# Reordering the prologue of a two-layer attention kernel, and spreading four sums over two units of products

## The chip, the cores and the metric

The kernel runs on one core of a Trainium2 chip. The metric is the device time of one execution in microseconds (us); the time of the kernel before is the median of three runs. Engines are named as in the profile: PE is TensorE (matrix products; PEld its weight loads), DVE is VectorE, ACT is ScalarE, POOL is GpSimd, and SP is the engine that issues most transfers (DMA). A "q" behind an engine's name (SPq, ACTq) is its queue of issued transfers.

## The reference

x has 8 images of 512 channels and 32x32 = 1024 positions, all in float32. Two attention layers follow each other. Cut to what matters:

```python
# layer 0: eight heads of 64 channels
hn  = group_norm(x, gn1_scale, gn1_bias)                 # 32 groups
qkv = einsum('bchw,oc->bohw', hn, w_qkv) + b_qkv         # 1536 x 512 weights
wgt = softmax(einsum('bct,bcs->bts', q * scale, k * scale))
a   = einsum('bts,bcs->bct', wgt, v)
out = group_norm(einsum('bchw,oc->bohw', a, w_proj) + b_proj, gn2_scale, gn2_bias)
x   = x + out
# layer 1: one head of 512 channels
w_qkv = g_qkv[:, None] * v_qkv / norm(v_qkv, axis=1)     # rows normalised
w_out = g_out[:, None] * v_out / norm(v_out, axis=1)
qkv = einsum('oc,bcn->bon', w_qkv, x)
qkv = qkv / (sqrt(mean(square(qkv), axis=1)) + 0.0001)
attn = softmax(einsum('bci,bcj->bij', q, k) * C ** -0.5)
h   = einsum('oc,bcn->bon', w_out, einsum('bij,bcj->bci', attn, v))
return (x + h) * 2 ** -0.5
```

## The kernel before

Channels lie on the 128 partitions in four blocks (ci = 0 to 3), so one image is a tile of 128 x 4 x 1024. The program is written out in full: the order of the calls is the order on each engine (class InOrder pins it), and each engine takes its own instructions strictly in that order. Buffers are the other thing that orders work. Seven large buffers are handed out by name (class Slots: a buffer given back goes to the end of a list, and the next taker waits for its last readers). The products' results go to PSUM: wide() gives one of three tiles of two banks, bank() one of two tiles of one bank, each in turn, and a new taker waits until the former result has been copied out. Each issued transfer also carries one of eight completion counters, and waits until the transfer that had this counter before has landed.

Layer 1 never forms q, k, v as such. Weights that do not depend on x are multiplied together once, in the prologue:

- score = wq' wk (product "pA", 16 products of 128x128 by 128x512, each done by PE in two passes), value = wv' wo' (product "pB", needs the transposed output weight woT), and gram = the sum over the 12 row tiles of w_qkv of rows' rows ("pG", upper blocks only: widths 512, 384, 256, 128), from which the mean square of qkv follows.
- score, value and layer 0's output weight are then cut into seven operands each (operands(): four sums on DVE, three copies on POOL, two transfers to a place in device memory, "far"), for a scheme that does a 2x2 block product with seven products in place of eight (class Seven).

The rows of layer 1's weights ("wrows", 16 tiles of 128x512: q, k, v, out) have to be normalised first: ACT squares a tile and sums it ("w"), DVE takes the inverse root by thirteen small steps (rsqrt_steps), multiplies it with g, and scales the tile.

Layer 0's weights come as rows and must be transposed (turn(): 16 products with the identity into two wide PSUM tiles, "wT_", half of each copied by DVE and half by ACT). The vectors (scales and biases) are loaded as rows of one small tile, and turned with one product ("pcol") into "cols".

The prologue before runs in this order: statistics of image 0 and its norm; turn v's weights (wT_v); half of v's projection (pv); turn k's and q's weights; first q and k projection (pqk), with the squares and the scaling of the w rows between; score (pA); turn woT; value (pB); operands; turn the projection (wT_p); its operands; gram (pG); store gram and fetch it again. Then the first scores of layer 0 ("s") begin. The loads are issued on SP: x, layer 0's rows, layer 1's rows in four transfers of 1 MB, the projection; the vectors on ACT.

For each image the heads of layer 0 follow (32 steps), its projection, and then layer 1: the products with gram (py), u = score times x (p_u, scaled on POOL by the inverse of the root mean square), v in four units of seven products (value_unit, p_v), and e, the exponents, in four units (weight_unit, p_e). weight_unit needs four sums of quarters of u (sum_u, tiles s12 and s34). A unit's products go in pairs into one wide tile, and after each second product Seven.drain() issues the additions that empty it. In the kernel before, sum_u puts its four sums on DVE in one go after the second of the four v units.

Of the kernel before, what the change touches and what calls it, by code (L numbers as in the profile page):

```python
# [8 lines left out]
F32 = mybir.dt.float32  # L9
# [43 lines left out]
def attention_blocks_kernel(  # L53
# [52 lines left out]
    def big(name, lead=CI):  # L106

        return slots.take([P, lead, CI * N // lead], name)
# [14 lines left out]
    def run(pieces):  # L123
        for _ in pieces:
            pass
# [10 lines left out]
        for hh in range(2):  # L136
            SY.dma_start(out=w0rows[t][hh * D : (hh + 1) * D], in_=w0v[t, hh])

    rows = const.tile([NCOLS, P], F32, name="rows")
    for r0, vec in (  # L140
        (G1S, gn1_scale), (G1B, gn1_bias), (BP, b_proj), (G2S, gn2_scale), (G2B, gn2_bias),
        (GQKV, g_qkv), (GOUT, g_out),
    ):
        n = vec.shape[0] // P
        AC.dma_start(out=rows[r0 : r0 + n, :], in_=vec.rearrange("(r p) -> r p", p=P))

    bv = b_qkv.rearrange("(j hh t d) -> t j hh d", hh=2, t=3, d=D)
    for t in range(3):
        for hh in range(2):
            AC.dma_start(out=rows[BQ + 4 * t : BQ + 4 * t + 4, hh * D : (hh + 1) * D], in_=bv[t, :, hh, :])  # L150

    def load_x(b, xt, ci):
        SY.dma_start(out=xt[:, ci, :], in_=xv[b, :, ci, :])
# [2 lines left out]
        load_x(0, x0, ci)  # L156
    for t in (2, 1, 0):
        load_w0(t)
    qk_rows, vo_rows = big("w1_qk", 2 * CI), big("w1_vo", 2 * CI)
    v1v = v_qkv.rearrange("(t j p) c -> t p j c", t=3, p=P)  # L160
    SY.dma_start(out=qk_rows[:, :CI, :], in_=v1v[0])
    SY.dma_start(out=qk_rows[:, CI:, :], in_=v1v[1])
    SY.dma_start(out=vo_rows[:, :CI, :], in_=v1v[2])
    SY.dma_start(out=vo_rows[:, CI:, :], in_=v_out.rearrange("(j p) c -> p j c", p=P))
    SY.dma_start(out=wprow, in_=w_proj.rearrange("(j p) c -> p j c", p=P))


    ident = const.tile([P, P], F32, name="ident")
# [62 lines left out]
    def fetch(name, b):  # L231
        SY.dma_start(out=place(name, b), in_=far[name])
# [488 lines left out]
    class Layer1:  # L721
# [10 lines left out]
        def project(self):  # L732
# [64 lines left out]
            def value_unit(m):  # L797

                w = near["value"]
                c = {f"{i + 1}{th + 1}": v[:, m + 4 * th, i * CH : (i + 1) * CH] for i in range(2) for th in range(2)}  # L800

                def last(which):
                    if which[0] == "1":
                        t = m + 4 * (which == "12")
                        AC.activation(v[:, t, :], v[:, t, :], AF.Copy, scale=rinv[:, t : t + 1])

                return Seven(
                    f"v_{b}_{m}", CH,
                    lambda k, h: w[:, k, h, :], self.right(slice(m * P, (m + 1) * P)), c, last, swap=True,
                )  # L810

            def sum_u():

                s12 = prob.tile([P, 2, 2, HN], F32, tag="p", name=f"s12_{b}")
                s34 = prob.tile([P, 2, 2, HN], F32, tag="p", name=f"s34_{b}")
                q1, q2 = halves_
                VE.tensor_add(s12[:, 0], u[:, :2, q2], u[:, 2:, q2])
                VE.tensor_sub(s12[:, 1], s12[:, 0], u[:, :2, q1])
                VE.tensor_sub(s34[:, 0], u[:, :2, q1], u[:, :2, q2])
                VE.tensor_sub(s34[:, 1], u[:, 2:, q1], s12[:, 1])  # L820
                self.s12, self.s34 = s12, s34
                for th in range(2):
                    e[th] = big(f"e_{b}_{th}", NT)
                    self.sums[th] = sum_pool.tile([P, HN], F32, tag="esum", name=f"esum_{b}_{th}")

            def weight_unit(m):

# [26 lines left out]
                        broadcast()  # L854
            if b + 1 < B:
                fetch("qk", b + 1)
            for m in range(4):
                run(value_unit(m).steps())
                if m == 1:
                    sum_u()  # L860
            if b + 1 < B:
                fetch("v", b + 1)
            for m in range(4):
# [25 lines left out]
                SY.dma_start(out=ov[self.b, :, c, :], in_=self.xt[:, c, :])  # L889


    place("qk", 0)
    place("v", 0)

    def turn_w0(t, name):
        near_t, far_t = (near["v"], far["v"]) if t == 2 else (near["qk"][:, t], far["qk"][:, t])
        turn(w0rows[t], near_t, name)
        SY.dma_start(out=far_t, in_=near_t)

    norm1 = Norm1(0, x0)  # L900
    for ci in range(CI):
        for k in range(2):
            norm1.stats(ci, k)
    pcol = bank("pcol", NCOLS)
    PE.transpose(pcol, rows, ident[:NCOLS, :NCOLS])
    VE.tensor_copy(cols, pcol)
    VE.tensor_scalar_mul(bqs, cols[:, BQ : BQ + CI], QSCALE0)
    VE.tensor_sub(bpd, cols[:, BP + 2 : BP + 4], cols[:, BP : BP + 2])
    norm1.means()
    norm1.gn.coeffs()  # L910
    for ci in range(CI):
        norm1.apply(ci, AC if ci % 2 else VE)
    turn_w0(2, "v")
    v0_0 = big("v0_0", NT)
    v0 = project_v0(0, x0, v0_0)
    for _ in range(NT // 2):
        next(v0)
    turn_w0(1, "k")
    turn_w0(0, "q")

    wrows = [qk_rows[:, j, :] for j in range(2 * CI)] + [vo_rows[:, j, :] for j in range(2 * CI)]
    nrm = [small.tile([P, 2 * CI], F32, tag="wn_n", name=f"wn_{k}") for k in range(2)]
    ss = [small.tile([P, 2 * CI], F32, tag="wn_ss", name=f"wss_{k}") for k in range(2)]

    def norm_rows(k):

        rsqrt(nrm[k], ss[k], 2 * CI, f"w1_{k}")
        VE.tensor_mul(nrm[k], nrm[k], cols[:, GQKV + 8 * k : GQKV + 8 * (k + 1)])
        for i in range(2 * CI):
            wrow = wrows[2 * CI * k + i]  # L930
            VE.tensor_scalar(wrow, wrow, nrm[k][:, i : i + 1], None, ALU.mult)

    qk0, todo = project_qk(0, 0, x0)
    for k in range(CI):
        next(todo)
        for i in range(CI * k, CI * (k + 1)):
            sq = prob.tile([P, C], F32, tag="p", name=f"w1_{i}")
            AC.activation(sq, wrows[i], AF.Square, accum_out=ss[i // 8][:, i % 8 : i % 8 + 1])
        if k % 2:
            norm_rows(k // 2)  # L940

    def prep_layer1():


        slots.give("rows_kq")
        woT = rows_vp[:, :CI, :]
        done1 = big("done1", 2 * CI)
        score, value = done1[:, :CI, :], done1[:, CI:, :]
        wq, wk, wv, wo = (wrows[k * CI : (k + 1) * CI] for k in range(4))

        def product(left, right, ci, c0, name):
            pm = bank(f"{name}_{ci}")
            run(matmuls(pm[:, c0:], [(l[:, ci * P : (ci + 1) * P], r[:, c0:]) for l, r in zip(left, right)]))
            return pm

        for ci in range(CI):
            VE.tensor_scalar_mul(score[:, ci, :], product(wq, wk, ci, 0, "pA"), QSCALE1)
        turn(vo_rows[:, CI:, :], woT, "o")
        for ci in range(CI):
            AC.copy(value[:, ci, :], product(wv, [woT[:, o, :] for o in range(CI)], ci, 0, "pB"))  # L960
        def operands(name, w, s7):

            q = [[w[:, 2 * j : 2 * j + 2, i * CH : (i + 1) * CH] for j in range(2)] for i in range(2)]
            op = [s7[i // 4][:, i % 4] for i in range(7)]
            VE.tensor_add(op[S1], q[1][0], q[1][1])
            VE.tensor_sub(op[S2], op[S1], q[0][0])
            VE.tensor_sub(op[S3], q[0][0], q[1][0])
            VE.tensor_sub(op[S4], q[0][1], op[S2])
            for i, part in ((A11, q[0][0]), (A12, q[0][1]), (A22, q[1][1])):
                PO.tensor_copy(op[i], part)  # L970
            SY.dma_start(out=far[name][:, :4], in_=s7[0])
            SY.dma_start(out=far[name][:, 4:], in_=s7[1][:, :3])

        for name, w, pool, tag in (("score", score, block, "pb"), ("value", value, prob, "p")):
            operands(name, w, [pool.tile([P, 4, 2, CH], F32, tag=tag, name=f"{name}7_{i}") for i in range(2)])
        slots.give("done1")
        done2, done3 = big("done2", 2 * CI), big("done3", 2 * CI)
        gram, proj = done2[:, :CI, :], done2[:, CI:, :]
        turn(wprow, proj, "p")
        d3 = done3.rearrange("p (k h) c -> p k (h c)", k=2).rearrange("p k (i h c) -> p k i h c", h=2, c=CH)  # L980
        operands("proj7", proj, [d3[:, k] for k in range(2)])

        VE.memset(gram, 0.0)
        for ci in range(CI):
            c0 = ci * P
            pg = product(wrows[: 3 * CI], wrows[: 3 * CI], ci, c0, "pG")
            VE.tensor_copy(gram[:, ci, c0 : c0 + P], pg[:, c0 : c0 + P])
            if c0 + P < C:
                VE.tensor_scalar_mul(gram[:, ci, c0 + P :], pg[:, c0 + P :], 2.0)
        SY.dma_start(out=far["gram"], in_=gram)  # L990
        SY.dma_start(out=far["proj"], in_=proj)
        for name in ("w1_qk", "w1_vo", "rows_vp", "done2", "done3"):
            slots.give(name)
        fetch("gram", 0)

    prep_layer1()


    heads = Heads(0, x0, v0_0, qk0)
# [133 lines left out]
```

## Time and profile before

| what | us |
|---|---|
| median of three runs | 3317.47 (3316.73 to 3318.27) |
| the profiled execution, its time | 3316.36 |
| its span (first to last instruction) | 3314.5 |
| PE busy | 3267.3 |
| DVE busy | 2117.2 |
| ACT busy | 1068.9 |
| POOL busy | 981.4 |
| first useful product of PE (wT_v) starts at | 16.56 |
| first scores (s) of layer 0 start at | 116.7 |

The span is a little shorter than the time; the difference, 1.9 us, lies around the program. A group's line gives the number of instructions, their busy time and mean, and the idle time of the engine just ahead of them with what ended it. A product's end is modelled (products overlap), so where the rate of PE matters, the distance between starts is used. The view of waits lists who waited for whom; the chain of waits follows the work that ended last back from step to step; the timeline gives start, duration and engine of each instruction in order. Nearly all instructions show one line, L34, since the recording class issues them all; they are told apart by the names of their tiles.

### The profile page before, as it was taken

Reading aid. Unit: us, or ns where it says so; the run is one execution under the profiler, and the core shown is the slowest. Engines: PE = TensorE matmul, PEld = TensorE weight load, DVE = VectorE, ACT = ScalarE, POOL = GpSimd, SP = SyncE. Lnnn points to the kernel's source line nnn. Section 1 sums busy time; section 2 is a strip of 40 time slices with the busy share of each in tenths; the row PEclk is TensorE's granted clock in tenths of the full one; section 3 lists DMA queues with packets and bytes.
Section 4 is the critical chain, followed back from the end, with each engine's and each line's share of the span. In section 5 each row is a group of like instructions: output and inputs, shape, how many; then the busy total and the mean of one; then the engine's idle time right before and its main releaser. Section 6 shows DMA issues by size and latency. Waiting matters only on the chain.

```text
span 3314.5 us, 35553 instructions
## 1 busy us (share of the span) xinstructions
PE 3267.3 (99%) x13177; PEld 1610.2 (49%) x13177; DVE 2117.2 (64%) x2830; ACT 1068.9 (32%) x1811; POOL 981.4 (30%) x855
## 2 busy tenths in 40 slices
PE   7999999999999999999999999999999999999899
PEld 3544544445444454544545445444454445444354
DVE  4596646965479654885448854497545966468653
ACT  2353123521145211451125512254122531235210
POOL 0253123521235112450224502254022531235111
PEclk9999999999999999999999999999999999999999
DMA  5586205752068410783117821287103862057600
GB/s 187 158 212 193 77 13 149 198 171 77 0 186 203 154 52 18 202 218 112 45 45 209 223 74 45 64 221 220 63 27 111 208 186 89 13 134 197 184 7 26
DMA packets 182659, 411.86 MB, mean 124 GB/s; under 512 B 27444, under 2 KB 27480, under 8 KB 176344
## 3 DMA queue, kind: packets, MB, share of 16 engines
q1 hardware_dynamic: 182368, 409.58, 43.5%
q8 instruction: 105, 1.72, 0.2%
q14 instruction: 66, 0.54, 0.0%
q10 hardware_dynamic: 120, 0.02, 0.0%
HBM read 113.53 MB, written 27.56 MB: 43 GB/s over the span
## 4 chain that ended last, share of the span: by engine, by line
PE 89%; DVE 4%; DMA 4%; SPq 2%; issue 1%; ACT 0%; DVEq 0%; POOL 0%; POOLq 0%
PE po L34 25%; PE s L34 12%; PE pqk L34 12%; PE pv L34 7%; PE p_e_T L34 7%; PE p_e_B L34 5%; PE py L34 4%; DMA pT<-pb 4%; PE p_u_T L34 3%; PE p_o_T L34 3%; PE p_v_T L34 3%; PE p_u_B L34 2%; PE p_o_B L34 2%; PE p_v_B L34 2%; DVE pb L34 2%; SPq L34 2%
## 5 line engine op out<-in xcount | busy, mean ns | idle before, releaser
L34 ACT ACTIVATE p<-s,nm 128x1024 f32<-128x1024 f32 x512 | 565.5, 1109 | 862.0 <-DVE nm L34 826.6
L34 POOL TENSOR_SCALAR p<-p,tt 128x1024 f32<-128x1024 f32 x512 | 565.9, 1118 | 927.6 <-DVE tt L34 924.2
L34 DVE TENSOR_REDUCE nm<-s 128x1 f32<-128x1024 f32 x512 | 602.2, 1218 | 175.0 <-PE s L34 174.3
L34 DVE STREAM_TRANSPOSE pb<-p 128x2048 f32<-128x2048 f32 x256 | 589.5, 2303 | 26.1 <-POOL p L34 16.4
L34 PE MATMUL s<-qk 64*128 64x512 f32 x2048 | 508.6, 602 | 0.0
L34 PE MATMUL po<-pT,v 128*64 128x256 f32 x4096 | 470.3, 382 | 4.7 <-DMA pT<-pb 3.5
L34 PE MATMUL pqk<-hn,qk 64*128 64x512 f32 (+1 forms) x2016 | 474.2, 591 | 0.0
L34 PE MATMUL po<-e,v 128*128 128x512 f32 x1024 | 450.9, 595 | 0.0
L34 PEld LDWEIGHTS po<-pT,v 128*64 128x64 f32 x4096 | 287.2, 137 | 216.6 <-ACT v L34 69.0
L34 PEld LDWEIGHTS pqk<-hn,qk 64*128 64x128 f32 (+1 forms) x2016 | 203.6, 187 | 250.2 <-issue 237.2
L34 PEld LDWEIGHTS po<-e,v 128*128 128x128 f32 x1024 | 192.2, 190 | 252.7 <-issue 245.5
L34 PEld LDWEIGHTS s<-qk 64*128 64x128 f32 x2048 | 195.0, 186 | 237.2 <-issue 231.3
L34 POOL TENSOR_TENSOR u<-u,xy 128x512 f32<-128x512 f32 x64 | 78.9, 1272 | 767.2 <-DMA xy<-far_rinv 590.4
L34 PE MATMUL pv<-v,hn 128*128 128x512 f32 x512 | 231.1, 603 | 1.4 <-ACT v L34 1.4
L34 DVE TENSOR_TENSOR e<-e,p_e_T 128x512 f32<-128x512 f32 x160 | 107.1, 686 | 145.0 <-PE p_e_T L34 142.8
L34 POOL TENSOR_TENSOR qk<-qk,v 128x512 f32<-128x512 f32 x124 | 158.4, 1277 | 83.9 <-ACT v L34 83.9
L34 ACT ACTIVATE e<-e,shift,rinv 128x512 f32<-128x512 f32 x128 | 100.9, 812 | 247.7 <-DVE e L34 247.7
L34 POOL TENSOR_TENSOR esum<-esum,e 128x512 f32<-128x512 f32 x96 | 121.5, 1266 | 164.0 <-ACT e L34 161.4
L34 PEld LDWEIGHTS pv<-v,hn 128*128 128x128 f32 x512 | 95.4, 192 | 118.2 <-issue 116.4
L34 PE MATMUL p_e_T<-s,t 128*128 128x512 f32 x320 | 147.8, 592 | 0.0
L34 PE MATMUL py<-x,gram 128*128 128x512 f32 x320 | 141.2, 601 | 6.0 <-issue 6.0
L34 DVE TENSOR_TENSOR v<-po,esum 128x512 f32<-128x512 f32 x56 | 38.7, 691 | 160.0 <-PE po L34 159.8
(184 smaller groups left out, 3059.0 us busy)
## 6 DMA issues: line engine op xcount, KB each, us to landing
pT<-pb SPq DMA_DIRECT2D x1024, 256.0 KB, 4.5
hn<-in_x_dram SPq DMA_DIRECT2D x32, 512.0 KB, 5.6
x<-in_x_dram SPq DMA_DIRECT2D x32, 512.0 KB, 5.9
out_dram<-x SPq DMA_DIRECT2D x32, 512.0 KB, 3.8
score<-far_score SPq DMA_DIRECT2D x8, 1792.0 KB, 7.4
value<-far_value SPq DMA_DIRECT2D x8, 1792.0 KB, 7.1
qk<-far_qk SPq DMA_DIRECT2D x7, 2048.0 KB, 7.8
proj<-far_proj SPq DMA_DIRECT2D x7, 1792.0 KB, 7.9
```

The lines of the kernel that those rows point to most:

```text
L34: return lambda *args, **kw: self._pin(call(*args, **kw))
```

## The change

In the prologue the order becomes: layer 1's rows are loaded first, in sixteen transfers of 256 KB, with only the two g vectors ahead on ACT; then x, layer 0's rows and the projection. The 16 row tiles are squared, normalised and scaled in five groups (2, 2, 4, 4, 4), and after each group PE adds its rows' part to all four blocks of gram, which are held in two wide PSUM tiles at once. The other vectors are loaded by ACT after the squares. Then come statistics of x, the turning of woT, score (pA) with the coefficients of the norm between, the turning of v's weights, value (pB), the turning of k's, v's projection, the turning of q's and of the projection, and the first q and k projection. So each turned weight is ready one stage ahead of its products. The norm is applied by POOL and DVE instead of ACT and DVE, score is copied from PSUM by ACT instead of DVE, the memory set of gram comes at the start, and gram stays where it is made: it is still stored, but not fetched.

In layer 1 the four sums of u are issued one by one, ahead of the additions of four different pairs, in the third and the fourth v unit.

The diff, cut to its core:

```diff
+    qk_rows, vo_rows = big("w1_qk", 2 * CI), big("w1_vo", 2 * CI)
+    wrows = [qk_rows[:, j, :] for j in range(2 * CI)] + [vo_rows[:, j, :] for j in range(2 * CI)]
+    g_rows = block.tile([4 * CI, P], F32, tag="pb", name="g_rows")
+    AC.dma_start(out=g_rows[: 3 * CI, :], in_=g_qkv.rearrange("(r p) -> r p", p=P))
+    AC.dma_start(out=g_rows[3 * CI :, :], in_=g_out.rearrange("(r p) -> r p", p=P))
...
+    for j in range(4 * CI):
+        SY.dma_start(out=wrows[j], in_=v1v[j] if j < 3 * CI else vov[j - 3 * CI])
...
-    SY.dma_start(out=qk_rows[:, :CI, :], in_=v1v[0])
-    SY.dma_start(out=qk_rows[:, CI:, :], in_=v1v[1])
-    SY.dma_start(out=vo_rows[:, :CI, :], in_=v1v[2])
-    SY.dma_start(out=vo_rows[:, CI:, :], in_=v_out.rearrange("(j p) c -> p j c", p=P))
...
-                VE.tensor_add(s12[:, 0], u[:, :2, q2], u[:, 2:, q2])
-                VE.tensor_sub(s12[:, 1], s12[:, 0], u[:, :2, q1])
-                VE.tensor_sub(s34[:, 0], u[:, :2, q1], u[:, :2, q2])
-                VE.tensor_sub(s34[:, 1], u[:, 2:, q1], s12[:, 1])
...
+                VE.tensor_add(s12[:, 0], u[:, :2, q2], u[:, 2:, q2])
+                yield
+                VE.tensor_sub(s12[:, 1], s12[:, 0], u[:, :2, q1])
+                yield
+                VE.tensor_sub(s34[:, 0], u[:, :2, q1], u[:, :2, q2])
+                yield
+                VE.tensor_sub(s34[:, 1], u[:, 2:, q1], s12[:, 1])
...
+            sums = sum_u()
             for m in range(4):
-                run(value_unit(m).steps())
-                if m == 1:
-                    sum_u()
+                for k, _ in enumerate(value_unit(m).steps()):
+                    if (m, k) in ((2, 0), (2, 4), (3, 1), (3, 5)):
+                        next(sums, None)
...
+    gram = place("gram", 0)
...
+    pcol = bank("pcol_g", 4 * CI)
+    PE.transpose(pcol, g_rows, ident[: 4 * CI, : 4 * CI])
+    VE.tensor_copy(cols[:, GQKV:], pcol)
...
+    VE.memset(gram, 0.0)
+    for lo, hi in ((0, 2), (2, 4), (4, 8), (8, 12), (12, 16)):
+        for i in range(lo, hi):
+            sq = prob.tile([P, C], F32, tag="p", name=f"w1_{i}")
+            AC.activation(sq, wrows[i], AF.Square, accum_out=ss[:, i : i + 1])
+        rsqrt(nrm[:, lo:hi], ss[:, lo:hi], hi - lo, f"w1_{lo}")
+        VE.tensor_mul(nrm[:, lo:hi], nrm[:, lo:hi], cols[:, GQKV + lo : GQKV + hi])
+        for i in range(lo, hi):
+            VE.tensor_scalar(wrows[i], wrows[i], nrm[:, i : i + 1], None, ALU.mult)
+            for ci in range(CI if i < 3 * CI else 0):
+                c0 = ci * P
+                PE.matmul(
+                    pg[ci][:, c0:], wrows[i][:, c0 : c0 + P], wrows[i][:, c0:], start=(i == 0), stop=(i == 3 * CI - 1)
+                )
+    load_vectors()
     norm1 = Norm1(0, x0)
...
+    norm1.aggregate()
+    pcol = bank("pcol", GQKV)
+    PE.transpose(pcol, rows, ident[:GQKV, :GQKV])
+    coeffs = norm1.gn.all_steps()
+    next(coeffs)
+    for ci in range(CI):
+        c0 = ci * P
+        VE.tensor_copy(gram[:, ci, c0 : c0 + P], pg[ci][:, c0 : c0 + P])
+        if c0 + P < C:
+            VE.tensor_scalar_mul(gram[:, ci, c0 + P :], pg[ci][:, c0 + P :], 2.0)
+    SY.dma_start(out=far["gram"], in_=gram)
+    VE.tensor_copy(cols[:, :GQKV], pcol)
...
+    turn(vo_rows[:, CI:, :], woT, "o")
+    for ci in range(CI):
+        AC.activation(score[:, ci, :], product(wq, wk, ci, "pA"), AF.Copy, scale=QSCALE1)
+        if ci == 1:
+            next(coeffs)
+            next(coeffs)
+    run(coeffs)
     turn_w0(2, "v")
+    for ci in range(CI):
+        norm1.apply(ci, PO if ci % 2 else VE)
+    operands("score", score, ...)
+    for ci in range(CI):
+        AC.copy(value[:, ci, :], product(wv, [woT[:, o, :] for o in range(CI)], ci, "pB"))
...
+    turn_w0(1, "k")
     v0_0 = big("v0_0", NT)
     v0 = project_v0(0, x0, v0_0)
     for _ in range(NT // 2):
         next(v0)
-    turn_w0(1, "k")
     turn_w0(0, "q")
+    operands("value", value, ...)
+    turn(wprow, proj, "p")
     qk0, todo = project_qk(0, 0, x0)
+    run(todo)
...
+    operands("proj7", proj, [d3[:, k] for k in range(2)])
+    SY.dma_start(out=far["proj"], in_=proj)
...
-        for ci in range(CI):
-            c0 = ci * P
-            pg = product(wrows[: 3 * CI], wrows[: 3 * CI], ci, c0, "pG")
...
-        fetch("gram", 0)
```

## The prediction

> **What bounds the kernel now.** I read the page's busy times first, then what TensorE waited for, in the whole span and in its first 122 us, then the chain of waits over that stretch, and last the timeline of one layer-1 stage.
>
> ```profile
> PE 3267.3 (99%) x13177; PEld 1610.2 (49%) x13177; DVE 2117.2 (64%) x2830; ACT 1068.9 (32%) x1811; POOL 981.4 (30%) x855
> ```
>
> TensorE (PE) is busy for all but 47 us, so time can only come from what it waits for. Its waits in the first 122 us (waited for: us, times, longest), with the layer-1 line from the whole span:
>
> ```profile
> PE pcol L34 <- DMA rows<-in_L_conv_b_qkv_dram: 10.5, 1, 10.5
> PE p_v_B L34 <- DVE v L34: 5.8, 8, 0.7
> PE wT_v L34 <- DMA rows_vp<-in_L_conv_w_qkv_dram: 2.1, 1, 2.1
> PE pA L34 <- DVE done L34: 1.5, 1, 1.5
> PE pv L34 <- ACT v L34: 1.4, 1, 1.4
> PE pB L34 <- ACT rows_vp L34: 1.4, 1, 1.4
> PE pA L34 <- ACT w L34: 1.3, 1, 1.3
> ```
>
> The chain of waits (start, us, what) shows how they follow each other:
>
> ```profile
> 16.56 3.66 PE wT_v L34 x16
> ...
> 21.61 16.06 PE pv L34 x32
> ...
> 41.16 13.75 PE pqk L34 x32
> ...
> 64.83 7.13 PE pA L34 x16
> ...
> 75.11 14.00 PE pB L34 x32
> ...
> 90.86 25.90 PE pG L34 x96
> 116.76 1.92 PE s L34 x8
> ```
>
> Real work starts only at 16.6 us. The first attention scores start at 116.7 us; from there on the two programs hold the same work. So the prologue's gain is the shift of that start.
>
> **Change 1, the prologue. When TensorE can start.** The Gram matrix needs row tiles 0 and 1 scaled by their norms. The first transfer of x, 512 KB, lands 3.8 us after its issue (4.5 us in the chain); tiles 0 and 1 are as many bytes in its place: 4.5. A square takes 0.62 and its sum 0.19: 5.3. That is not the last to come. g_rows' second transfer stands where one of the small vectors was issued at 1.32; the issue queued behind that one's counter began at 4.36, so it lands at about 4.3. Then its turn on TensorE and the way to VectorE (DVE), 0.63 as from pm (12.40) to mean (13.03); the copy, 0.2; the new MEMSET of gram ahead of the norms, 1.76 by the old MEMSET; thirteen norm steps and the product with g, 2.83 (51.23 to 54.06); the first row's scale, 0.48. Sum: 4.3+0.63+0.2+1.76+2.83+0.48 = 10.2, so TensorE starts at 10.3. With 2 us of doubt in g_rows' landing this is 9 to 12.
>
> **Does the supply keep up?** One row tile is 8 of the 96 passes: 25.90/12 = 2.16 us. On DVE each group costs 2.83 us and 0.41 a row: rows 2 and 3 are ready at 14.0 and 14.4, rows 4 to 7 by 19, 8 to 11 by 23.5, 12 to 15 by 28. TensorE needs row 2 not before 14.7, row 4 not before 19, row 8 not before 27.5, even were its clock full from the start. No wait. For the loads: row 7 must land by about 15. The slices of the DMA view before and after 25 us read
>
> ```profile
> 20.00:25.00 5.00, 3.60 (x5) 1.50 (x5) 0.69 (x1) 1.26 (x3) 0.00 (x0) 1.00 1.08 215
> 25.00:30.00 5.00, 5.00 (x12) 2.23 (x11) 0.00 (x0) 0.00 (x0) 0.00 (x0) 1.00 1.04 366
> ```
>
> (last column GB/s). By 25 us 5.4 MB have moved, x and the 64-partition pieces of w_qkv; the 128-partition rows of layer 1 come after. At 366 GB/s a tile of 262 KB takes 0.7 us and row 7 lands near 9; at 215 it takes 1.2 and lands near 12.5.
>
> Here a rule speaks against the change: the Trainium skill, "DMA: Bandwidth & Descriptors", section "Rules for kernel authors", wants at least 1 MiB in a transfer, and the change cuts four such loads into sixteen of 256 KB. The same page fits 2.0 us fixed plus bytes/436 GB/s (for GpSimd's path). If sixteen paid that one after another, my estimate is 42 us for the rows, and x behind them at about 55: statistics and pm would then come at 58 and not at 39, and the prologue would lose 6 us instead of gaining. But the row for small transfers is
>
> ```profile
> pT<-pb SPq DMA_DIRECT2D x1024, 256.0 KB, 4.5
> ```
>
> 1024 of them, 4.5 us to landing each, and four are issued for each 2.3 us transposition: they overlap. I take the trace.
>
> **The cold clock.** In the first five pairs of pv, starts lie 0.855 us apart, later 0.43:
>
> ```profile
> 22.62 0.33 PEld L34 LDWEIGHTS pv<-v,hn 128*128 128x128 f32 x1 [0.52 <-issue]
> ...
> 26.34 0.19 PEld L34 LDWEIGHTS pv<-v,hn 128*128 128x128 f32 x1 [0.24 <-issue]
> ```
>
> so pv takes 16.06 instead of 13.75, 2.3 us more; wT_v ahead of it took 3.66 where later turns take 1.75. The skill's "TensorE: Matmul & The Clock Gate", Part 1, gives half clock for the first 3.4 us or so of sustained work, that is 1.7 us lost, and lets it return after an idle window as long. I take the row, 2.3, now paid by the Gram matrix; wT_v, no longer first, is warm and saves 1.9. By the rule the end would be 0.6 earlier.
>
> **TensorE's new order, by starts:** 10.3; Gram 25.9+2.3 → 38.5; pcol and pm 0.5 → 39.0 (DVE is through with x's eight statistics by 33.5: 28.0, 8 of 0.64, 0.42; the vectors, issued by ACT after the 16th square and, the last six, after the second tile of x has landed, are there by 22 to 31); wT_o 1.75 → 40.7 (its second half needs pG's buffer: seven copies of gram, 0.2 to 0.55, begin as pG's first tile ends, done for that tile at about 39.6, nothing lost); pA 13.75, pv 0.25 and a new wait: the third pA takes the bank that pv leaves, freed by ve, 0.8 after pv begins as before (13.83 to 14.62) → 55.5; wT_v 1.75 → 57.3; pB 13.75 → 71.0; wT_k 1.75, pv 13.75, wT_q and wT_p 3.5, pqk 13.75 → 103.8. Behind the new wait stand only TensorE's own later products; its 0.8 is in the sum.
>
> The three waits ahead of pA and pB (1.3, 1.5, 1.4) and the one ahead of pv go, because woT is turned before pA, v's weights before pB, k's before pv. What each of the moved copies hides behind: wT_o's copies behind pA, wT_v's behind pB, the four applications of the norm (two now on GpSimd (POOL), 1.1 each by its 128x1024 row, in ACT's place) behind pB as well, the score and value operands behind pB and pqk. The closest of these is wT_p: DVE is about at 93 with its copies, ACT's evacuation of pqk starts then, and the third pqk wants its bank at 96.7. Were that cover gone it would cost what ACT is late. SP's queue: rows_kq is issued behind four of the b_qkv transfers, by 31 at worst, and needed at 71; far_score, far_value and far_proj leave before 98, while the first turned block of scores is issued near 109. Leaving out gram's fetch and the wait for its store frees SP near the first block; nobody waits for it in the trace, so nothing.
>
> Gain: 116.7 − 103.8 = 12.9 us.
>
> **Change 2, u's sums.** In the timeline of the first image (start, us, engine):
>
> ```profile
> 411.75 1.22 DVE L34 TENSOR_TENSOR s<-u 128x1024 f32<-128x1024 f32 x1
> ...
> 416.48 0.41 DVE L34 TENSOR_TENSOR v<-v,p_v_B 128x256 f32<-128x256 f32 x1
> 416.95 1.99 PE L34 MATMUL p_v_B<-value,x 128*128 128x256 f32 x8 [0.73 <-DVE v L34]
> ```
>
> four sums in a row hold DVE for 4.7 us, and TensorE, whose three pair buffers give it 2 × 1.73 us of lead, stops. The stop costs more than 0.73: v's 28 products run from 398.79 to 423.96 = 25.17 us, and undisturbed starts lie 0.863 apart, 24.17 in all. So 1.0 an image, 8.0 for eight. After the change each pair has at most one sum in front of its additions. Counting from the end of unit 1 with pairs of 1.73 us: sums end at 1.5, 5.7, 8.7 and 13.0, the pairs' additions at 2.4, 4.5, 7.0, 7.5, 9.7, 11.8, 13.9; the pair that reuses a buffer starts at 5.2, 6.9, 8.7, 10.4, 12.1, 13.8: each is free at least 1.6 us before. The first sum waits for no one: POOL ends u's scaling at 407.8. The last sum is needed by the sixth product of the next unit, 8 us on. I take the whole 8.0; bounds 0 (the stop moves to another pair) and 8.0 (none is left).
>
> **Sum.** The profiled execution took 3316.36, its span 3314.5 and 1.9 around it. 3314.5 − 12.9 − 8.0 = 3293.6; with 1.9, 3295.5. The median of the runs shown is 1.1 above the profiled one: 3296.6.
>
> **The rivals.**
> *The sums only move the stop.* For: DVE would be busy for 11.5 of 12.1 us in units 2 and 3. Against: the slack of 1.6 us above. 3317.5 − 12.9 = 3304.6.
> *The Gram starts late or in pieces,* by slow first loads or g_rows held up behind 4 MB of rows: TensorE starts at 14 to 18 instead of 10.3. For: the b_qkv vectors landed only at 10.5. Against: they were issued until 7.3, so even they took 3.2. Gain 13 to 17: about 3302.
> *Slower: x comes too late.* It now queues behind 4.2 MB of rows, and TensorE stops at pm, in front of all that is left. Each us after 39 costs one; from 60 on both gains are gone. That needs 6.3 MB to move at less than 110 GB/s, half of the slowest stretch seen; or the single-file price above. At 64 us it gives 3322.
> *It doesn't do what it says:* were the program's order the old one, 3317.5; but the built order of instructions has the Gram products first and the sums apart.
>
> **How the numbers follow.** Forecast 0.74, stop moved 0.10, late start 0.08, x late 0.04, some other loss that leaves it within the measurement 0.04. About 0.2% (6.6 us) is what a measurement of this kernel can tell from no change. The forecast's own range is 3292 to 3300 (start 9 to 12, cold clock 1.7 to 2.3, the copies); with the stop moved and the late start the 80% range is 3291.5 to 3305. Faster 0.92, same 0.04, slower 0.04.
>
> **What would show it.** The first pG at 10 to 11 us and no wait inside it; scores first at 104 ± 2; no wait longer than 1 us for TensorE before that; no p_v wait. Wrong if pm or pcol waits for x or the vectors, if starts of pG stay 0.85 apart past 16 us, or if TensorE waits in weight units for S4.

## The result, and the profile after

The changed kernel takes 3295.51 us, the median of six runs (3294.1 to 3295.85). Six runs of the kernel before beside it have a median of 3315.82 (3313.75 to 3318.27). The ratio is 0.9938, with a 95% interval of 0.9925 to 0.9951: faster by 0.6%, and clear of the 0.2% that the forecast set as its bound. The forecast was 3296.6.

The profiled execution took 3295.35 and its span is 3293.2 us, 21.3 shorter than before. Busy times of the page of after:

```profile
PE 3263.8 (99%) x13178; PEld 1606.6 (49%) x13178; DVE 2118.5 (64%) x2869; ACT 1071.5 (33%) x1813; POOL 983.4 (30%) x857
```

TensorE does the same work. What changed is its waits. In the first 110 us the list of its waits (waited for: us, times, longest) now has three entries:

```profile
PE pG L34 <- DVE w_qk L34: 5.5, 1, 5.5
PE pcol_g L34 <- DMA g_rows<-in_L_conv_g_out_dram: 4.0, 1, 4.0
PE pA L34 <- DVE ve L34: 0.3, 1, 0.3
```

The first two are the empty stretch until the Gram products can start; the 10.5, 2.1, 1.5, 1.4, 1.4 and 1.3 of before are gone (with 1.6 at pm and 0.8 at pv, two lines of that list which the forecast left out), and of p_v, 5.8 in eight images, no line is left in the list of the whole span. The chain of waits of after (start, us, what) over the same stretch:

```profile
1.40 2.48 DMA g_rows<-in_L_conv_g_out_dram
...
4.86 1.76 DVE gram L34
...
9.78 27.64 PE pG L34 x96
...
37.91 1.80 PE wT_o L34 x16
...
46.59 0.13 PE pv L34 x2
...
46.96 7.13 PE pA L34 x16
...
55.84 13.73 PE pB L34 x32
...
71.32 13.74 PE pv L34 x32
...
88.55 13.73 PE pqk L34 x32
102.28 1.92 PE s L34 x8
```

From the first Gram product to the first scores TensorE's work follows on without a gap but for the 0.4 between pv at 46.59 and pA at 46.96. The scores start at 102.28 where they started at 116.76: 14.5 us. From the scores to the end the program is then 6.8 us shorter as well (3293.2 − 102.28 against 3314.5 − 116.76). That is the sums, less some small waits further down. In the timeline of the first image in layer 1 (start, us, engine):

```profile
397.27 1.22 DVE L34 TENSOR_TENSOR s<-u 128x1024 f32<-128x1024 f32 x1
...
400.85 1.22 DVE L34 TENSOR_TENSOR s<-s,u 128x1024 f32<-128x1024 f32 x1
...
403.85 1.22 DVE L34 TENSOR_TENSOR s<-u 128x1024 f32<-128x1024 f32 x1
...
408.09 1.22 DVE L34 TENSOR_TENSOR s<-u,s 128x1024 f32<-128x1024 f32 x1
```

The four sums lie 3.0 to 4.2 us apart, and TensorE's products on either side read

```profile
384.32 1.03 PE L34 MATMUL p_v_B<-value,x 128*128 128x256 f32 x4
...
408.49 1.88 PE L34 MATMUL p_e_B<-u,x 128*128 128x512 f32 x4
```

From v's first product to e's first are 24.17 us, where the kernel before has 25.17. By starts it is so in each of the eight images.

### The profile page after: what moved, and what is told of

Same layout as the page of the kernel before. It is cut to its first block, busy times and chain, and to the rows that moved or that the text cites. A ratio compares the mean times of both kernels' runs of the same rounds, so it can differ in the third digit from the quotient of the medians.

```text
span 3293.2 us, 35605 instructions
## 1 busy us (share of the span) xinstructions
PE 3263.8 (99%) x13178; PEld 1606.6 (49%) x13178; DVE 2118.5 (64%) x2869; ACT 1071.5 (33%) x1813; POOL 983.4 (30%) x857
## 4 chain that ended last, share of the span: by engine, by line
PE 94%; DVE 2%; DMA 2%; SPq 1%; issue 1%; DVEq 0%; ACTq 0%
PE po L34 26%; PE s L34 13%; PE pqk L34 12%; PE pv L34 7%; PE p_e_T L34 7%; PE p_e_B L34 5%; PE py L34 4%; PE p_u_T L34 3%; PE p_v_T L34 3%; PE p_o_T L34 3%; PE p_v_B L34 3%; PE p_u_B L34 3%; PE p_o_B L34 2%; DMA pT<-pb 1%; DVE pb L34 1%; PE pG L34 1%
```

## The experiments

One table holds them; "first pG" and "first s" are starts in us, "pG" the time from its first start to the next product. They are from the chain of waits, or, for the kernels with unused turns and with 13 unused products (and pG of those with 15 and with late turns), from the timeline, where s and the product behind pG read 0.07 less. The chain puts pG of the kernel before 0.17 late: by starts alone pG takes 25.99 there and 27.57 in after. "Clock opens" is the moment at which the trace of the execution records that TensorE's granted clock rises from half to full for the first time. Median and ratio stand where a kernel was timed several times; the other rows are one execution each.

| kernel | first pG | pG | clock opens | first s | span | median | ratio to before |
|---|---|---|---|---|---|---|---|
| before | 90.86 | 25.90 | 25.78 | 116.76 | 3314.5 | 3315.82 | |
| after | 9.78 | 27.64 | 12.79 | 102.28 | 3293.2 | 3295.51 | 0.9938 (0.9925 to 0.9951) |
| after, once more | 9.85 | 28.61 | 14.83 | 103.32 | 3293.0 | 3295.40 | 0.9935 (0.9922 to 0.9949) |
| sums alone | 91.93 | 25.90 | 26.27 | 117.83 | 3307.8 | 3308.28 | 0.9976 (0.9967 to 0.9986) |
| prologue alone | 9.90 | 28.48 | 14.63 | 103.25 | 3302.7 | 3303.52 | 0.9961 (0.9947 to 0.9975) |
| three sums, then one | 9.81 | 28.52 | 14.62 | 103.20 | 3295.1 | | |
| turns late | 9.94 | 28.8 | 15.46 | 113.78 | 3304.1 | | |
| memory set on POOL | 8.27 | 28.93 | 13.89 | 102.06 | 3291.3 | | |
| the same, loads of 1 MB | 11.38 | 28.43 | 16.00 | 104.67 | 3293.3 | | |
| x loaded first | 13.72 | 27.82 | 17.09 | 106.41 | 3297.6 | | |
| unused products | 9.81 | 26.16 | 7.14 | 100.83 | 3291.5 | | |
| unused turns | 9.85 | 27.8 | 6.97 | 102.5 | 3291.7 | | |
| POOL, 15 unused products | 8.7 | 26.0 | 8.03 | 99.60 | 3289.9 | 3291.88 | 0.9931 (0.9917 to 0.9944) |
| POOL, 13 unused products | 8.31 | 27.0 | 10.12 | 100.15 | 3290.9 | 3292.48 | 0.9926 (0.9914 to 0.9939) |

The column of first s tells more about the prologue than the span does: later small waits, at the transposed blocks pT in the last image above all, differ between executions. From first s to the end the kernels with spread sums took 3188.6 to 3191.9.

### One half at a time

The kernel before with nothing but the spread sums:

```diff
             for m in range(4):
-                run(value_unit(m).steps())
-                if m == 1:
-                    sum_u()
+                for k, _ in enumerate(value_unit(m).steps()):
+                    if (m, k) in ((2, 0), (2, 4), (3, 1), (3, 5)):
+                        next(sums, None)
```

> The kernel before with only u's sums spread. My theory (the two changes add up): the eight p_v waits go, v's 28 products take 24.2 us by starts as in the changed kernel, span 3314.5 - 8.0 = 3306.5, ratio 0.9976; the first scores stay at 116.7 us. Rival (the sums' stop only showed because of the prologue, or moves elsewhere): span within 2 us of 3314.5.

And the changed kernel with the four sums in one go again:

```diff
-                for k, _ in enumerate(value_unit(m).steps()):
-                    if (m, k) in ((2, 0), (2, 4), (3, 1), (3, 5)):
-                        next(sums, None)
+                run(value_unit(m).steps())
+                if m == 1:
+                    sum_u()
```

> The changed kernel with u's four sums in one go again. My theory: first scores at 102.2 us, 14.5 earlier than before, and eight p_v waits of 0.73 (1.0 us each by starts); span about 3293.2 + 8.0 = 3301.2 at most, ratio about 0.9957. Rival (the prologue's gain is partly given back later): ratio above 0.998.

Measured ratios are 0.9976 and 0.9961; their product is 0.9937, beside 0.9938 for both together. So the two parts add, and neither gives back what the other brings. (With the sums alone the first scores came at 117.83, not at 116.7, since the first weights landed later; with the prologue alone they came at 103.25, not at 102.2. Both spans are 1.3 to 1.5 above the expected ones.) With the sums alone no wait for p_v is left; with the prologue alone the line is back, in the list of TensorE's waits, unchanged to the tenth:

```profile
PE p_v_B L34 <- DVE v L34: 5.8, 8, 0.7
```

The sums' 8 us are more than these 5.8, as the count by starts had it: each wait of 0.73 delays the starts by 1.0.

### How much slack the sums have

Three sums ahead of one pair, and the fourth where it was:

```diff
-                    if (m, k) in ((2, 0), (2, 4), (3, 1), (3, 5)):
+                    if (m, k) == (2, 0):
+                        for _ in range(3):
+                            next(sums, None)
+                    if (m, k) == (3, 5):
                         next(sums, None)
```

> The changed kernel with three sums ahead of the third unit's first additions and the fourth where it is. My count of slack: three sums end where four had ended 1.22 us later, and the stop was 1.0 by starts, so no p_v wait at all (0.2 us to spare) and v's products in 24.2 us as with single sums. Rival (each sum needs a pair of its own): p_v waits remain, 0.3 us or more in each image.

No wait for p_v appears. The span is 1.9 longer than after's: 0.9 has arisen by the first scores, all of it in pG (28.52 against 27.64, as the clock opened later), and one wait for a pT block is 1.5 longer than after's (4.3 against 2.8). In each image v's products take 24.17, as with single sums. So three sums together, 3.7 us of DVE, still fit into the lead that TensorE's three pair buffers give; the fourth is the one that does not. The spreading over four pairs, rather than the parting of the fourth from three, buys nothing that this run shows.

### What the turns one stage ahead are worth

woT's turn was put right ahead of pB, v's right ahead of its projection, and k's behind that one:

```diff
-    turn(vo_rows[:, CI:, :], woT, "o")
...
-    turn_w0(2, "v")
     for ci in range(CI):
         norm1.apply(ci, PO if ci % 2 else VE)
     operands("score", score, ...)
+    turn(vo_rows[:, CI:, :], woT, "o")
...
-    turn_w0(1, "k")
+    turn_w0(2, "v")
     v0_0 = big("v0_0", NT)
...
+    turn_w0(1, "k")
     turn_w0(0, "q")
```

> The changed kernel with each weight turned right ahead of its products again: woT after pA, v's weights ahead of pv, k's and q's ahead of pqk. My theory: TensorE waits 1.4 us for the copies of woT ahead of pB and as long ahead of pv, about 1.7 each by starts; pqk waits for nothing since k's turn comes before q's. First scores at 102.2 + 3.3 = 105.5 us. Rival (the order of the turns is worth nothing here, the gain came from the early start alone): 102.2.

The direction is right and the size is far off: the scores start 11.5 us after those of after (113.78 − 102.28), not some 3. The chain of waits of this kernel:

```profile
54.91 0.60 ACT done L34
...
55.54 0.70 DVE score L34
...
56.26 2.60 DVE score L34 x3
58.86 0.61 DVE done L34
...
60.09 0.59 ACT done L34
...
60.73 16.93 PE pB L34 x32
77.66 1.76 PE wT_v L34 x16
...
80.81 14.00 PE pv L34 x32
```

Score and woT both show under the buffer's name "done". DVE's copy of woT's first half (58.86) stands behind the four sums that make the score operands, and these behind ACT's copy of the last score block (54.91). So TensorE waits for 4.1 us, not for 1.4 as in the kernel before, where the operands came only after pB. The size is thus that of this order, operands before turn, and not of a late turn alone. The slices of this kernel by windows (busy us of PE, PEld, DVE, ACT and POOL with their numbers of instructions, then the granted clock, DMA share, GB/s) show a second price:

```profile
59.00:60.00 1.00, 0.00 (x0) 0.00 (x0) 1.00 (x2) 0.50 (x1) 0.00 (x0) 0.92 0.99 410
60.00:61.00 1.00, 0.27 (x1) 0.27 (x2) 0.06 (x1) 0.67 (x2) 0.00 (x0) 0.50 0.97 393
...
66.00:68.00 2.00, 2.00 (x5) 0.91 (x4) 0.00 (x0) 0.58 (x1) 0.00 (x0) 0.84 0.00 0
```

The clock falls to half at about 59.8, some 3.2 us into the gap (turns end at 56.6), and until 66.66 it stays there, so that pB runs its first 6 us at half rate: 16.93 instead of 13.73. Of the 11.5, then, 7.3 is pB's wait and its cold clock; 1.7 is v's projection (wait 1.4, and 14.00 against 13.74); 2.5 had arisen by the end of pA, mostly from a colder Gram stage (1.2 longer by starts) and a wait of 0.9 for the cols, which wT_o no longer covers.

### The start: memory set, size of the loads, order of the loads

gram's memory set on POOL instead of DVE:

```diff
-    VE.memset(gram, 0.0)
+    PO.memset(gram, 0.0)
```

> The changed kernel with the memory set of gram on GpSimd. My theory: it stood on the path to the first Gram product; the norm steps then start when the second square's sum is there, at 5.0 us and not at 6.5, the first pG at 8.2 instead of 9.8, first scores at 100.7 instead of 102.2. Rival (the path waits for the loads or for g): 9.8 and 102.2 as they are.

That, and layer 1's rows again in four transfers of 1 MB:

```diff
-    for j in range(4 * CI):
-        SY.dma_start(out=wrows[j], in_=v1v[j] if j < 3 * CI else vov[j - 3 * CI])
+    SY.dma_start(out=qk_rows[:, :CI, :], in_=v4[0])
+    SY.dma_start(out=qk_rows[:, CI:, :], in_=v4[1])
+    SY.dma_start(out=vo_rows[:, :CI, :], in_=v4[2])
+    SY.dma_start(out=vo_rows[:, CI:, :], in_=v_out.rearrange("(j p) c -> p j c", p=P))
```

> As memset_away, but layer 1's rows in four transfers of 1 MB as in the kernel before. My theory: nothing is gained by the large transfers, and the first two tiles wait for a whole 1 MB: it lands at about 5.8 us, first pG at about 10.6 instead of 8.2, first scores at 103. Rival (small transfers waste bandwidth, as the rule on 1 MiB has it): all 4 MB are there clearly earlier than with sixteen, and the first scores are no later than 100.7.

And after with x's four transfers moved ahead of the rows:

> The changed kernel with x loaded ahead of layer 1's rows. My theory: 2.1 MB of x at some 300 GB/s push row tile 1 to about 10.6 us, first pG to 14.6 instead of 9.8, first scores to 107. Rival (the rows' place in the queue hardly matters, since TensorE has other limits): first scores within 1 us of 102.2.

The starts of pG came within 0.9 us of those expected: 8.27, 11.38 and 13.72. With 1 MB the first transfer lands 5.94 after its issue, the first tile can be squared only then, and the Gram starts 3.1 later than with tiles of 256 KB. With x first the first row tile lands at 8.96. At the first scores the cut of the loads is worth 2.6 us (104.67 against 102.06) and their order 4.1, and TensorE waits for nothing in the supply after the first product in either (the same 0.3 at pA is left).

The earlier start by the memory set did not arrive, however. First pG is 1.5 earlier than in after, first scores 0.2, not 1.5. The Gram products themselves took 28.93 instead of 27.64. In the timeline of weight loads of this kernel:

```profile
8.27 0.50 PEld L34 LDWEIGHTS pG<-w_qk 128*128 128x128 f32 x2 [4.16 <-DVE w_qk L34]
...
13.55 0.34 PEld L34 LDWEIGHTS pG<-w_qk 128*128 128x128 f32 x1 [0.52 <-issue]
14.15 1.49 PEld L34 LDWEIGHTS pG<-w_qk 128*128 128x128 f32 x7 [0.26 <-issue]
```

and in that of after:

```profile
11.65 0.33 PEld L34 LDWEIGHTS pG<-w_qk 128*128 128x128 f32 x1 [0.52 <-issue]
12.29 0.33 PEld L34 LDWEIGHTS pG<-w_qk 128*128 128x128 f32 x1 [0.31 <-issue]
12.87 0.85 PEld L34 LDWEIGHTS pG<-w_qk 128*128 128x128 f32 x5 [0.24 <-issue]
```

A load of 0.34 with 0.52 of idle ahead of it is the cold pattern. With the memory set on POOL it is still there 5.3 us after the first product, and the clock opens at 13.89, after 5.6 us. In after the loads are quick from 12.87, and the clock opens at 12.79, after 3.0 us. The difference of 2.6 at half rate is the 1.3 by which pG is longer. So the earlier start did bring its 1.5 us, and a clock that opened later took 1.3 of it back. The rest of the experiments are about this.

### The cold clock

The question is whether any work of TensorE opens the clock. First, unused products of the identity with itself while TensorE waits, 4 ahead of g's turn and 14 behind it (they add work; nothing uses their result):

```diff
+    spin(4)
     pcol = bank("pcol_g", 4 * CI)
     PE.transpose(pcol, g_rows, ident[: 4 * CI, : 4 * CI])
+    spin(14)
```

> The changed kernel with 18 products of the identity by itself, not used, on TensorE while it waits: 4 ahead of g's turn, 14 behind it. My theory (the first 3.4 us or so of sustained work run at half clock, whoever does them): the Gram products run at full clock from the start, 25.9 us instead of 27.6, first scores 1.7 us earlier, at 100.5. Rival (the slow start of pG is its own, by loads of weights or by waits for rows): 27.6 and 102.2 as they are.

Then the same with 8 and 20 turns (transpositions) in place of products:

> As warm_matmul, but with 28 turns of the identity (TensorE's transposition) in place of the products: 8 ahead of g's turn, 20 behind it. In the kernel before 3.7 us of turns ran ahead of pv and pv still began at half clock. Theory A (turns do not count as work for the clock): the Gram products take 27.6 us as in the changed kernel, first scores at 102.2. Theory B (they count, and before it was the gap of 1.4 us behind them that let the clock fall): 25.9 and 100.5.

With products pG takes 26.16, by starts 0.1 more than in the kernel before, where it stands warm; the first scores come at 100.83. With turns it takes 27.8, as in after. That looks as if turns did not open the clock (theory A), but the trace says otherwise. The turns start 0.21 us apart until 6.87 and 0.11 apart from 7.03, and the clock opens at 6.97, when TensorE has done nothing but turns. It then falls again, as the weight loads of pG show:

```profile
9.85 0.30 PEld L34 LDWEIGHTS pG<-w_qk 128*128 128x128 f32 x2 [2.12 <-DVE w_qk L34]
...
11.22 0.34 PEld L34 LDWEIGHTS pG<-w_qk 128*128 128x128 f32 x1 [0.52 <-issue]
...
14.23 0.19 PEld L34 LDWEIGHTS pG<-w_qk 128*128 128x128 f32 x1 [0.24 <-issue]
```

pG begins at full rate; the granted clock is 0.50 from 10.38 to 13.79 and full again from there. So turns count (theory B). The clock fell after 3.41 us of which TensorE had stood idle for 1.9, between the turns and pG; with the products that gap was 0.8, and the clock stayed.

The three changes lie at 6.97, 10.38 and 13.79, each 3.41 us after the last. In the kernel with late turns they lie at 15.46, 59.83 and 66.66, which is 13 and 2 times 3.41. In all fourteen traces the changes within one execution lie whole multiples of 3.41 us apart. So the clock is set anew only at the marks of such a grid, and the two traces of the changed kernel (12.79 and 14.83, no whole step apart) show that the grid stands elsewhere in each execution. It also fits that the 3.66 us of turns in the kernel before opened nothing: counted back from the 25.78 there, marks fell at 18.96 and 22.37, and in the step that ended at each of them TensorE had stood idle for about 1 us or more.

Then both moves at once, the memory set on POOL and 4 + 11 unused products, and the same with 4 + 9, beside the changed kernel once more:

> Both at once: the memory set of gram on GpSimd and 15 unused products of the identity while TensorE waits. If the two add up: first pG at 8.2, Gram products in 25.9 us, first scores at 102.2 - 1.6 - 1.7 = 98.9, span about 3290. If the unused products overrun, pG starts later than 8.3.

> The memory set of gram on POOL and unused products of the identity with itself ahead of the Gram products, now four before the turn of g and nine behind it instead of eleven, so that TensorE is free before the first row is scaled (8.3 us). Theory (the unused products open the clock, the moved memory set brings the start forward, and the two add up): first pG at 8.3 to 8.4, pG 25.9 long, scores at 99.1, a span of about 3289.5 and a median of about 3291.5, ratio to the kernel before 0.9929. Rival (with fewer unused products, or with a gap behind them, the clock is not open when the Gram products begin): pG 27 to 28 long, scores at 100.5 to 101.5, median 3293.

> The changed kernel unaltered, on the same chip and in the same rounds, so that the warmed version can be told from it. Theory: median 3295.5, ratio to the kernel before 0.9938, 4 us slower than the warmed version; first pG at 9.8. Rival (the warmed version's gain lies within the scatter of small waits later on): the two medians lie within 2 us of each other. In either case the length of pG here, 27.6 to 28.5, shows how much the cold clock scatters for one and the same program.

The unused products of the first one ran 0.4 too long (first pG at 8.7, not 8.3) but left the clock open: pG 26.0. With two fewer pG started at 8.31 and took 27.0. In its timeline of weight loads

```profile
9.32 0.34 PEld L34 LDWEIGHTS pG<-w_qk 128*128 128x128 f32 x1 [0.52 <-issue]
...
11.88 0.19 PEld L34 LDWEIGHTS pG<-w_qk 128*128 128x128 f32 x1 [0.24 <-issue]
```

the clock opens at 10.12, 6 us after TensorE's unbroken work began. In the kernels with 18 and with 15 unused products that work began at much the same moment (4.0 to 4.2) and the clock opened at 7.14 and 8.03. So it is the grid that made the difference here, and not the two products fewer. The rival of that expectation came true for pG, and the median came out between theory and rival. Beside it the changed kernel unaltered has 3295.40 (3293.82 to 3296.22) and the warmed one 3292.48 (3290.62 to 3294.01): 2.9 us apart, with ranges that overlap by 0.2. The traces agree, 3.1 us at the first scores. It is the better kernel of the two, but by 0.09%, less than the 0.2% by which the forecast told change from no change.

The two traces of the changed kernel itself differ by 0.97 in pG (27.64 and 28.61) and by 1.04 at the first scores. That is the clock again: it opened 3.0 and 5.0 us after the first product. So one trace cannot tell a gain of a microsecond in this stage: the memory set moved away, without warming, shows 0.2 against the first trace of after and 1.3 against the second, and it was run only once.

## Why the prediction was right

**Start of TensorE, put at 10.3 (9 to 12): 9.78.** The terms hold one by one, and one was not in the sum: 0.4 of idle on DVE between the copy and the memory set. g_rows landed at 3.9 instead of 4.3; its turn and copy end at 4.5; the memory set took 1.76, the norm steps 2.7 instead of 2.83, the first scale 0.5. g's way and the memory set, and not the loads, set this start, as the sum had it: the memory set moved away brings it to 8.27.

**No stop in the supply: right.** The list of waits has none for pG but the first. A slice of after shows the loads: columns as above.

```profile
10.00:12.00 2.00, 2.00 (x3) 0.95 (x4) 1.67 (x11) 2.00 (x7) 0.00 (x0) 1.00 1.05 398
```

The rows, and x behind them, came at 297 to 310 GB/s in the first microseconds and at 380 to 407 from 6 to 16; 366 had been assumed. The Trainium skill's rule of at least 1 MiB ("DMA: Bandwidth & Descriptors", "Rules for kernel authors") was weighed, and the trace preferred; here the measurement differs from the rule twice. The kernel with 1 MB transfers moved no more in the same slices (373 to 413 from 6 to 16 us, against 358 to 411 with 256 KB and the same memory set), and it started later. x, now last, was no rival: its statistics were through by 31.9, against 37.4 when TensorE asked for them.

**Cold clock, put at 2.3: 1.74 in this trace** as the table reads it, 1.58 by starts, and 2.56 in the second trace of the same kernel. That the Gram stage would pay it was right; its size is not one number. The forecast weighed one from a row against one from a rule, and the quantity is neither: it is half of the time from the first product to the mark at which the clock opens. Over the seven kernels that go cold into pG that time was 3.0 to 5.6 us, and pG took 1.6 to 2.9 longer than 25.99; each loss is within 0.1 of the half. The Trainium skill, "TensorE: Matmul & The Clock Gate", Part 1, says that the window over which activity is watched, 3.4 us, is free-running, and the grid of 3.41 in the traces agrees. If a whole window had to be busy, the cold time would be anything from one window to nearly two (it is an estimate from the page). Six of the eight traces lie within that, and x loaded first, with 3.37, at its edge. In after the clock opened sooner, although TensorE had stood idle for the first 0.4 of the 3.4 us before 12.79. So 1.7, which the forecast took from the rule, is near the lower end, and how much of a window must be busy is not shown. Where the grid stood in an execution was luck, for this forecast too.

**The new wait at the third pA, put at 0.8: 0.4.** In the chain pv begins at 46.59 and the third pA at 46.96; the buffer was free after 0.17 of DVE's work. The 0.8 of the old order ran from pv's start, so the sum, which adds pv's 0.25 as well, counts that piece twice; and pv ran cold there (its copy ve began 0.63 after it).

**Scores at 103.8: 102.28.** The 1.5 us are the terms above: 0.5 from the start, 0.6 from the clock, 0.4 from the wait. The gain of the prologue is 14.5 for a predicted 12.9; up to a whole microsecond of that is the luck of the clock, as the second trace (103.32) shows.

**The moved copies at nothing: right here,** and the closest of them, wT_p's ahead of the third pqk, shows no wait either. What their cover is worth was told wrongly in the expectation of the late-turn kernel, which took the waits of before for it: with the operands in front one of them grew to 4.1 and threw the clock back for 3.2 more.

**The sums, 8.0: right.** The slack counted by hand was right as well. Counted from the end of unit 1 (384.32 + 14 × 0.863 = 396.4), the sums end at 2.1, 5.7, 8.7 and 12.9; predicted were 1.5, 5.7, 8.7 and 13.0. Of the 8.0 the span shows 6.8. Periods from one image's layer 1 to the next one's are shorter by 0.9 to 1.0 in four of seven images; the periods of the others differ by 0.3, 0.4 and 1.7, in small waits that also differ between traces of one kernel. In the last image one wait of 2.8 for a pT block let the clock fall, and 32 products took 5.18 instead of 3.67. By medians the sums alone brought 8.0 (3316.29 to 3308.28).

The sum: 14.5 + 6.8 = 21.3, for 12.9 + 8.0 = 20.9 predicted. An excess of 1.6 in the first term and a want of 1.2 in the second cancel, so the total is nearer than its parts.

None of the rivals came. Late x and a moved stop would each have left a line in the list of waits, and there is none; a late start would have put the first pG at 14 to 18.

## What to carry to other kernels

Where the busiest engine waits at the start, take the stage whose inputs need the least time from the first transfer, and put each step that another engine has to finish one stage ahead of where it is used; price such a step by everything that stands in front of it in the other engine's queue, not by the step alone. A long run of work for a helper engine that stalls TensorE need only be cut below TensorE's lead in free buffers: three sums fit, four did not. Before a gain of a microsecond at the start is believed, look at two traces of one kernel, since the moment of the clock's opening alone moved it by that much.

## What the runs showed of the hardware

TensorE's clock changed only at marks 3.41 us apart, which stand elsewhere in each execution: two traces of one kernel were cold for 3.0 and 5.0 us of their first stage, and lost half of that.

A gap of 4.1 us in TensorE's work cost 3.2 us beyond itself, in the half clock after it, and the clock fell some 3.2 us into the gap. A gap of 1.9 us, ahead of pG in the kernel with unused turns, made it fall as well, for 3.4 us. Gaps of 1.4 us behind warm stages (ahead of pB in before, of pv with late turns) cost 0.3 or less.

The column of the granted clock shows such a fall (0.50), but it reads 1.00 in the cold stretches at the start, in before from 22 to 25.8 us and in after from 10 to 12.8, where starts of products of full width lie 0.855 us apart. It counts the clock as full until the first change on record. At the start of a program the moment of that change, the distance of starts, or the 0.52 of idle between weight loads tells the cold clock.

Unused products can open it, at no price as long as TensorE has nothing else to do, and turns can too: 15 or 18 products saved 1.5 to 1.7 us of pG, compared with 27.64. With 13 of them, in an execution whose clock opened only at 10.12, it was about 0.7.

And the recorded wait understates a stop: 0.73 recorded, 1.0 in the distance of starts.
